# Projections of attention blocks as four products of 32 columns each, on a Trainium2 core

## Chip, cores and metric

The kernel runs on one NeuronCore of a Trainium2 chip, in one launch. The metric is the device time in microseconds (us) from start to end of one execution; several runs of the same kernel are shown with their median. The engines are named as in the profile: PE is TensorE (matrix products; PEld is its loading of weights), DVE is VectorE, ACT is ScalarE, POOL is GpSimd and SP is SyncE, which issues the transfers.

## What is computed

The reference applies four transformer blocks, one after the other, to `x` of 16 batches by 256 tokens by 256 channels, in float32, with 16 heads of 16 channels. A context of 77 tokens a batch serves the cross attentions. The third of the four blocks shows the pattern; the others leave out parts of it or differ in norms, gates, masks and rotary embeddings.

```python
def _L2_xcond_ref(x, c, context, ...):
    shift_a, scale_a, gate_a, shift_m, scale_m, gate_m = split(silu(c) @ W_mod + b_mod, 6)
    qkv = modulate(_ln(x), shift_a, scale_a) @ W_qkv + b_qkv
    ...
    attn_out = softmax(q @ k.T * scale) @ v                 # per batch and head
    x = x + gate_a[:, None] * (attn_out @ W_proj + b_proj)
    q_c = _ln(x) @ W_qc + b_qc                              # cross attention
    k_c, v_c = split(_ln(context) @ W_kvc + b_kvc, 2)
    ...
    x = x + (c_attn_out @ W_cproj + b_cproj)
    h = gelu(modulate(_ln(x), shift_m, scale_m) @ W_mlp1 + b_mlp1)
    return x + gate_m[:, None] * (h @ W_mlp2 + b_mlp2)

x = _L0(x); x = _L1(x); x = _L2(x); x = _L3(x)
```

Block L0 has self attention with rotary embedding and a mask over the 256 by 256 scores, a cross attention and an MLP. L1 is one cross attention. L2 is shown. L3 has rotary embedding in both of its attentions. That makes seven attentions a batch, three self (256 keys) and four cross (77 keys), and three MLPs.

## The kernel before

All of `x` stays in SBUF. The work runs in six stages: attention of L0 (weights "a"), its MLP ("b"), attention of L1 and L2 ("c"), the MLP of L2 ("d"), attention of L3 ("e"), its MLP ("f"). An MLP waits for all exponentials of the attention stage ahead of it.

An attention of one batch goes like this. The norm's result is turned into `xT` (channels on partitions, two chunks of 128 by 256 tokens). Projections follow:

- without rotary embedding, `project_T` (L615) makes queries and keys transposed: for each group `g` of 128 output channels and each chunk `k` of input channels one product of a weight block (128 by 128) with `xT` (128 by 256);
- with rotary embedding, `rotate_tasks` (L652) makes them with tokens on partitions (L671); DVE and POOL rotate them, and `turn_back` (L711) transposes them on PE;
- `mmv` (L782) makes the values, tokens on partitions;
- `residual` (L983) is the product after attention and also the MLP's second product; `nk` is 2 for the first and 8 for the second. It adds to `x` on DVE or POOL.

In cross attentions, keys and values come from the 77 context tokens, so their products are 77 wide or 77 high.

Scores are made twice: rows (L828, L840) for a maximum on DVE, and transposed (L922), from which ACT makes the exponentials `ec` (L936). Both use row tiling: four head pairs lie in the four 32-partition strips, and each strip's product takes 32 rows of the array and 128 columns. The masked ones of L0 also add the mask with 64 by 64 products (L915). The sum of values over keys, `values` (L945), uses the other tiling: the exponentials are the moving operand with 128 (or 77) rows, and the values of a head pair are 32 columns, so four head pairs lie in the four column strips of the array and write the four 32-partition strips of one PSUM bank. Projections, transposes and MLP use the whole array.

Every float32 product shows in the trace as two records (two passes) on PE, each with its weight load.

The order on all engines is written out by a planner before the program is built. `Order.add` takes a task with its engine, an estimated duration, the tasks it depends on, and the buffers (`Hold`s) that it takes and uses; `Order.solve` plays the tasks through in time and starts on each engine what is ready, has room for its buffers and has the best priority. On PE it adds a cost when the kind of task differs from that of the one before:

```python
TURN = {"row": 0.2, "col": 0.13}
...
kind = "row" if ts[0].rp is not None else ts[0].kind
dur += self.TURN.get(kind, 0.2) if kind != mode else 0.0
```

Score tasks count as "row", `values` tasks as "col"; projections have no kind. The product of 128 by 128 by 256 has an estimated duration `MM` of 0.432 us.

Buffers matter for one part of the change. There are eight PSUM banks ("b"), two sets of exponentials ("ec") and two of attention results ("oT"). In `attention`, `open_e` (L895) opens the exponentials of head group `g` and key chunk `kc`; the one with `g` and `kc` both 0 also takes the block's oT, which the later `back` fills and `residual` reads.

Of the kernel before, what the change touches and what calls it, by code (L numbers as in the profile page):

```python
# [17 lines left out]
P = 128  # L18
NT = N // P
NC = D // P  # L20
# [53 lines left out]
class Order:  # L74
# [10 lines left out]
    def add(self, eng, dur, run, deps=(), take=(), use=(), prio=0, rp=None, kind=None, more=0.0,  # L85
            lat=0.0, first=False, mb=0.0):

        t = Task()
        t.more, t.lat, t.first, t.mb = more, lat, first, mb
        t.eng, t.dur, t.run, t.prio, t.rp, t.kind = eng, dur, run, prio, rp, kind  # L90
        t.deps = [d for d in deps if d is not None]
        t.take, t.held = list(take), list(take) + list(use)
        for h in t.held:
            h.users += 1
        t.outs, t.left, t.ready, t.no, t.since = [], len(t.deps), 0.0, len(self.tasks), None
        for d in t.deps:
            d.outs.append(t)
        self.tasks.append(t)
        return t
# [95 lines left out]
def pixart_kernel(ctx: ExitStack, tc: tile.TileContext, x, cond_t, ctx_in, mask_c, mask_s, tables, vecs, rows,  # L195
                  mod0, mod1, mod2, mod3, wa, wb, wc, wd, we, wf, out):
    nc = tc.nc
# [26 lines left out]
    def buf(h, tag=None):  # L224

        return pools[tag or h.tag][h.no]

    def psum(h, *dims):

        t = banks[h.no]  # L230
        return t.rearrange("p (a b) -> p a b", a=dims[0]) if dims else t
# [380 lines left out]
        return s, last, hc  # L612


    def project_T(dst, w, xT):  # L615

        for g in range(NC):
            for k in range(NC):
                nc.tensor.matmul(dst[:, g, :], lhsT=w[:, k, g * P:(g + 1) * P], rhs=xT[:, k, :],
                                 start=(k == 0), stop=(k == NC - 1))  # L620
# [31 lines left out]
    def rotate_tasks(s, key, ws, xT, src_t, n, half, uses, name, prio):  # L652


        nt = (n + P - 1) // P
        r = min(n, P)
        width = len(ws) * D
        out_t, hold = [], []
        for group in ([list(range(nt))] if len(ws) == 1 else [[t] for t in range(nt)]):
            hm, hr, hq, u = Hold("b"), Hold("rope"), Hold("qk"), {}  # L660
            nm = f"{key}_{name}_{group[0]}"
            w_all = len(group) * width

            def mm(group=group, u=u, hm=hm, hq=hq):
                u["p"] = psum(hm)
                u["r1"] = s[key, group[0]] = buf(hq)
                for i, t in enumerate(group):
                    for j, w in enumerate(ws):
                        at = (i * len(ws) + j) * D
                        for k in range(NC):  # L670
                            nc.tensor.matmul(u["p"][0:r, at:at + D], lhsT=xT()[:, k, t * P:t * P + r],  # L671
                                             rhs=w()[:, k, :], start=(k == 0), stop=(k == NC - 1))

            def turns(group=group, u=u, hr=hr):
                r1 = u["r1"]
                r2 = u["r2"] = buf(hr)
                hn = width // HD
                for i, t in enumerate(group):
                    tt = (t * P % half) // P
                    pv, v1, v2 = (a[0:r, i * width:(i + 1) * width].rearrange("q (h w) -> q h w", w=HD)  # L680
                                  for a in (u["p"], r1, r2))
                    cs = tabT[0:r, tt, 0, :].unsqueeze(1).to_broadcast([r, hn, HD])
                    nc.vector.tensor_tensor(v1, pv, cs, ALU.mult)
                    for z in range(2):
                        sn = tabT[0:r, tt, 1, 8 * z:8 * z + 8].unsqueeze(1).to_broadcast([r, hn, 8])
                        nc.vector.tensor_tensor(v2[:, :, 8 * z:8 * z + 8], pv[:, :, 8 - 8 * z:16 - 8 * z], sn,  # L686
                                                ALU.mult)

            def plus(u=u, w_all=w_all):
                r1 = u["r1"][0:r, 0:w_all]  # L690
                nc.gpsimd.tensor_tensor(r1, r1, u["r2"][0:r, 0:w_all], ALU.add)  # L691
            size = len(group) * len(ws)
            a = add("PE", size * NC * MM, mm, deps=[src_t], take=[hm, hq], use=uses, prio=prio)
            d = add("DVE", 0.75 * size, turns, deps=[a, tab_t], take=[hr], use=[hm, hq], prio=prio)
            out_t.append(add("POOL", 0.65 * size, plus, deps=[d], use=[hr, hq], prio=prio))
            hold.append(hq)
        return out_t, hold, nt, r
# [18 lines left out]
    def attention(b, name, n, wv, wkeys, h_w, w_t, eps, mod, half, biases, masked, pre_add, gate, prio, ctxs=None,  # L716
# [31 lines left out]
        if half is None:  # L748
            hm1, hm2, u = Hold("b"), Hold("b"), {}

            def mmq():
                u["q"] = psum(hm1, NC)
                project_T(u["q"], wv[kq], s["xT"])

            def mmk():
                p = psum(hm2)
                u["k"] = p[:, 0:NC * n].rearrange("p (c n) -> p c n", n=n)
                project_T(u["k"], wv[kk], src())
            a = add("PE", (4 * MM) if self_ else 1.0, mmk, deps=[*src_t, w_t[kk], late_t], take=[hm2], use=[h_kq, *h_src, *h_w],
                    prio=prio)  # L760
            k_t = take_k(s, bk, n, lambda: u["k"], a, [hm2, h_kq], prio)
            a = add("PE", 4 * MM, mmq, deps=[xT_t, w_t[kq], late_t], take=[hm1], use=[h_kq, hx, *h_w], prio=prio)
            q_t = take_q(s, bq, lambda: u["q"], a, [hm1, h_kq], prio)
        elif self_:
            info = rotate_tasks(s, "qk", [lambda: wv[kq], lambda: wv[kk]], lambda: s["xT"],
                                add("NO", 0.0, lambda: None, deps=[xT_t, w_t[kq], w_t[kk]], prio=prio), N, half,
                                [hx, *h_w], nm, prio)
            q_t = turn_back(s, "qk", 0, info, lambda *z: take_q(s, None, *z), h_kq, f"q{nm}", prio)
            k_t = turn_back(s, "qk", D, info, lambda *z: take_k(s, None, n, *z), h_kq, f"k{nm}", prio)
        else:  # L770
            info = rotate_tasks(s, "kr", [lambda: wv[kk]], src, add("NO", 0.0, lambda: None, deps=[*src_t, w_t[kk]],
                                                                   prio=prio), n, N, [*h_src, *h_w], nm, prio)
            k_t = turn_back(s, "kr", 0, info, lambda *z: take_k(s, None, n, *z), h_kq, f"k{nm}", prio)
            info = rotate_tasks(s, "qr", [lambda: wv[kq]], lambda: s["xT"],
                                add("NO", 0.0, lambda: None, deps=[xT_t, w_t[kq]], prio=prio), N, half, [hx, *h_w],
                                nm, prio)
            q_t = turn_back(s, "qr", 0, info, lambda *z: take_q(s, None, *z), h_kq, f"q{nm}", prio)
# [4 lines left out]
        def mmv():  # L782
            ps = uv["p"] = psum(hm3)
            xT = src()
            for t in range(nk):
                for k in range(NC):
                    nc.tensor.matmul(ps[0:rows_n, t * D:(t + 1) * D], lhsT=xT[:, k, t * P:t * P + rows_n],  # L787
                                     rhs=wv[kv][:, k, :], start=(k == 0), stop=(k == NC - 1))

        def take_v():  # L790
# [2 lines left out]
            pairs = pairs.rearrange("p t h (a w) -> p t h a w", w=HD)  # L793
            for t in range(nk):
                nc.scalar.copy(pairs[:, t, :, 0:4:3, :], pv[:, t].rearrange("p (h i) w -> p h i w", i=2))
        a = add("PE", nk * NC * MM, mmv, deps=[*src_t, w_t[kv]], take=[hm3], use=[h_v, *h_src, *h_w], prio=prio)
        v_t = add("ACT", 0.37 * nk, take_v, deps=[a, ones_t], use=[hm3, h_v], prio=prio)


# [90 lines left out]
        for g in range(NC):  # L890
            u5, avs, h_av, h_so = {}, [], Hold("b"), Hold("ts")
            for kc in range(nk):
                h_e, ex = Hold("ec"), []

                def open_e(g=g, kc=kc, h_e=h_e):  # L895
                    if g == 0 and kc == 0:
                        s["oT"] = buf(h_ot)
                    for r in range(4):
                        s["e", g, kc, r] = buf(h_e)[:, r]
                t_e = add("NO", 0.0, open_e, deps=[qx_t, v_t, barrier], take=[h_e] if g or kc else [h_e, h_ot],  # L900
                          prio=prio)
                for rp in (1, 0):
                    hs = [Hold("b"), Hold("b")]
# [79 lines left out]
    def residual(s, b, deps, lhsT, w, nk, holds, gate, name, prio, after=None):  # L983
# [3 lines left out]
        for t in range(NT):  # L987
            def mm(t=t):
                if t == 0:
                    u["p"] = psum(hm, NT)  # L990
                for k in range(nk):
                    nc.tensor.matmul(u["p"][:, t, :], lhsT=lhsT(k, t), rhs=w()[:, k, :], start=(k == 0),  # L992
                                     stop=(k == nk - 1))
            ts.append(add("PE", nk * MM, mm, deps=[*deps, *ts], take=[hm] if t == 0 else [],
                          use=holds if t == 0 else [hm, *holds], prio=prio))
        if gate is None:
            def plus():
# [359 lines left out]
```

## Time and profile before

| | |
|---|---|
| time, median of three runs | 2632.84 us (2628.79 to 2638.83) |
| profiled execution: its time, its span | 2631.43 us, 2629.7 us |
| instructions in the span | 56144 |
| granted TensorE clock, mean | 0.995 |
| PE records of scores: L828, L840, L922 | 1536, 2048, 5120 |
| PE records of values: L945 | 5120 |
| PE records of projections with a 128 by 128 weight: L619, L671, L787, L992 | 640, 640, 384, 896 |
| PE records of the MLPs: L1035, L992 | 1536, 1536 |
| ACT exponentials, L936: count, mean of one | 1152, 596 ns |

A line in a list of the trace names the line of the kernel, engine and operation, what is written and read, the size and the count. In the timeline, lines begin with the start and the length of a merged piece; the ends of PE's products are modelled and reach into the next product, so the spacing of starts tells more of PE than its busy time. A line of waits has the total, the number and the longest.

### The profile page before, as it was taken

Reading aid. Unit: us, or ns where it says so; the run is one execution under the profiler, and the core shown is the slowest. Engines: PE = TensorE matmul, PEld = TensorE weight load, DVE = VectorE, ACT = ScalarE, POOL = GpSimd, SP = SyncE. Lnnn points to the kernel's source line nnn. Section 1 sums busy time; section 2 is a strip of 40 time slices with the busy share of each in tenths; the row PEclk is TensorE's granted clock in tenths of the full one; section 3 lists DMA queues with packets and bytes.
Section 4 is the critical chain, followed back from the end, with each engine's and each line's share of the span. In section 5 each row is a group of like instructions: output and inputs, shape, how many; then the busy total and the mean of one; then the engine's idle time right before and its main releaser. Section 6 shows DMA issues by size and latency. Waiting matters only on the chain. (4 is left out here: it accounts for less than half of the span.)

```text
span 2629.7 us, 56144 instructions
## 1 busy us (share of the span) xinstructions
PE 2575.5 (98%) x21512; PEld 1813.2 (69%) x21512; DVE 1627.7 (62%) x4537; ACT 1255.4 (48%) x2511; POOL 1113.5 (42%) x1413
## 2 busy tenths in 40 slices
PE   8999999999999899999999999999999999999999
PEld 5555565666888666666666667888666666666888
DVE  7888886676131577777777775111888887885100
ACT  2444455664333456555556654322455555554322
POOL 5233333558452355233334656442333324657310
PEclk9999999999999899999999999999999999999999
DMA  5000101223321121111111113111100001122110
GB/s 171 30 27 29 34 25 39 73 80 101 100 78 54 40 70 54 48 55 40 39 40 38 61 62 114 64 54 45 35 28 30 28 24 37 50 66 71 56 57 29
DMA packets 159749, 143.10 MB, mean 54 GB/s; under 512 B 24648, under 2 KB 124216, under 8 KB 158712
## 3 DMA queue, kind: packets, MB, share of 16 engines
q1 hardware_dynamic: 159480, 139.51, 16.9%
q8 instruction: 169, 2.77, 0.4%
q14 instruction: 100, 0.82, 0.1%
HBM read 91.86 MB, written 47.61 MB: 53 GB/s over the span
## 5 line engine op out<-in xcount | busy, mean ns | idle before, releaser
L936 ACT ACTIVATE ec<-bank 128x512 f32<-128x512 f32 (+1 forms) x1152 | 608.5, 596 | 514.0 <-PE bank L828 260.7
L922 PE MATMUL bank<-kq 32*128 32x256 f32 (+1 forms) x5120 | 627.9, 395 | 4.8 <-DMA kq<-mrow 4.4
L491 POOL TENSOR_SCALAR xn<-x_sb,mv,rstd 128x256 f32<-128x256 f32 x320 | 451.1, 1464 | 108.4 <-DVE y L519 97.8
L922 PEld LDWEIGHTS bank<-kq 32*128 32x128 f32 (+1 forms) x5120 | 357.2, 167 | 172.8 <-issue 105.1
L828 PE MATMUL bank<-kq 32*128 32x512 f32 x1536 | 432.5, 633 | 2.4 <-ACT ec L936 2.4
L858 DVE TENSOR_REDUCE mx<-bank 128x2 f32<-128x512 f32 x544 | 341.6, 681 | 46.0 <-PE bank L828 43.7
L945 PE MATMUL bank<-ec,v 128*32 128x256 f32 (+1 forms) x5120 | 347.9, 385 | 5.8 <-ACT ec L936 3.6
L1040 ACT ACTIVATE ec<-bank,vec 128x256 f32<-128x256 f32 x384 | 159.7, 467 | 401.3 <-PE bank L1035 373.2
L1035 PE MATMUL bank<-xT,kq 128*128 128x256 f32 x1536 | 341.4, 379 | 0.0
L992 PE MATMUL bank<-kq,ec 128*128 128x256 f32 x1536 | 339.7, 379 | 0.0
L992 PEld LDWEIGHTS bank<-kq,ec 128*128 128x128 f32 x1536 | 291.5, 190 | 39.5
L1035 PEld LDWEIGHTS bank<-xT,kq 128*128 128x128 f32 x1536 | 290.5, 190 | 40.4 <-issue 1.6
L967 POOL TENSOR_TENSOR od<-ts,rec 128x128 f32<-128x128 f32 x448 | 170.1, 402 | 318.7 <-DVE rec L961 318.1
L519 DVE STREAM_TRANSPOSE y<-xn 128x512 f32<-128x512 f32 x158 | 110.9, 702 | 298.9 <-DMA yd<-y 257.6
L945 PEld LDWEIGHTS bank<-ec,v 128*32 128x32 f32 (+1 forms) x5120 | 137.2, 109 | 183.0 <-issue 75.5
L862 DVE TENSOR_REDUCE mx<-bank 128x4 f32<-128x308 f32 x512 | 211.9, 468 | 55.4 <-PE bank L922 25.3
L466 POOL TENSOR_SCALAR rstd<-mv 128x2 f32<-128x2 f32 x160 | 37.5, 235 | 423.8 <-DVE mv L461 347.7
L854 DVE CUSTOM_DVE_ANT_0 junk<-bank,ctx 128x256 f32<-128x256 f32 x448 | 188.8, 421 | 45.2 <-PE bank L828 12.2
L954 DVE STREAM_TRANSPOSE ts<-bank 128x512 f32<-128x512 f32 x224 | 158.3, 707 | 76.6 <-PE bank L945 69.1
L691 POOL TENSOR_TENSOR qk<-qk,rope 128x512 f32<-128x512 f32 (+1 forms) x96 | 112.9, 1178 | 194.4 <-DVE rope L686 151.3
L1008 POOL TENSOR_TENSOR x_sb<-x_sb,tmp 128x512 f32<-128x512 f32 x80 | 101.6, 1270 | 179.4 <-DVE tmp L1005 179.2
L840 PE MATMUL bank<-kq 32*128 32x154 f32 x2048 | 167.1, 308 | 1.5 <-DVE ts L954 0.5
(164 smaller groups left out, 3437.8 us busy)
## 6 DMA issues: line engine op xcount, KB each, us to landing
yd<-y SPq DMA_DIRECT2D x158, 256.0 KB
xr<-yd SPq DMA_DIRECT2D x158, 256.0 KB
kq<-in_mod_dram SPq DMA_DIRECT2D x10, 512.0 KB
cin<-in_ctx_in_dram SPq DMA_DIRECT2D x36, 128.0 KB
x_sb<-in_x_dram SPq DMA_DIRECT2D x16, 256.0 KB
gb<-gate_g0m SPq DMA_DIRECT2D x16, 256.0 KB
gb<-gate_g2a SPq DMA_DIRECT2D x16, 256.0 KB
gb<-gate_g2m SPq DMA_DIRECT2D x16, 256.0 KB
```

Source lines behind the costliest of these rows:

```text
L491: nc.gpsimd.tensor_scalar(to, of, s["mv"][:, t, 0:1], s["rstd"][:, t:t + 1], ALU.subtract, ALU.mult)
L828: ls.append(lambda ps=ps, R=R, keys=keys: nc.tensor.matmul(ps.rearrange("p (s k) -> p s k", k=N), lhsT=s["qx"][R, 0, g, t * P:(t + 1) * P] ...
L840: ls.append(lambda ps=ps, R=R, keys=keys, tt=tt: nc.tensor.matmul(ps[:, 2 * tt * n:2 * (tt + 1) * n].rearrange("p (s k) -> p s k", k=n), l ...
L854: nc.vector.tensor_tensor_reduce(junk, u[i][:, i2 * N:(i2 + 1) * N], mb[:, t, :], -1.0, 3.0e38, ALU.add, ALU.min, m[:, i2, g, t:t + 1])
L858: nc.vector.tensor_reduce(m[:, :, g, t], u[i].rearrange("p (s k) -> p s k", k=N), AX.X, ALU.max, negate=True)
L862: nc.vector.tensor_reduce(m[:, :, g].rearrange("p s t -> p t s"), u[i][:, 0:4 * n].rearrange("p (t s k) -> p t s k", s=2, k=n), AX.X, ALU. ...
L922: (lambda ps=u[i], R=R, q=q: nc.tensor.matmul(ps[0:rows_n, q * N:(q + 1) * N], lhsT=s["kz"][R, q, g, kc * P:kc * P + rows_n], rhs=s["qx"][ ...
L936: nc.scalar.activation(e, u[i][0:rows_n], AF.Exp)
L945: nc.tensor.matmul(u5["p"][32 * r:32 * r + 32, 1 - q, :], lhsT=s["v"][0:rows_n, kc, 8 * g + 2 * r + 1 - q, :], rhs=s["e", g, kc, r][0:rows ...
L967: nc.gpsimd.tensor_tensor(ov[:, :, HD * i:HD * i + HD], ts[:, i, :, HD * i:HD * i + HD], rec[:, i, :].unsqueeze(2).to_broadcast([P, N // 3 ...
L992: nc.tensor.matmul(u["p"][:, t, :], lhsT=lhsT(k, t), rhs=w()[:, k, :], start=(k == 0), stop=(k == nk - 1))
L1035: nc.tensor.matmul(u["p"][:, j, :], lhsT=wv["w1"][:, k, f * P:(f + 1) * P], rhs=s["xT"][:, k, :], start=(k == 0), stop=(k == NC - 1))
```

## The change

Projections with a full set of 128 columns in the attention blocks are made as four products of 32 columns each, in the four column strips that `values` uses. The new helper `strips` runs over the chunks of input channels (`pairs`), and within each over the four slices `J` of 32 columns of the stationary operand; each writes its 32 partitions of the same destination. It is called in `project_T` (except for keys of the 77 context tokens), in `rotate_tasks` (except for these), in `mmv` for self attention, and in `residual` for attention (`nk == NC`). The products with 77 tokens, the transposes and the MLPs stay as they are.

The tasks concerned get `kind="col"`, so the planner counts 0.13 us for them instead of 0.2 after a task of another kind and nothing after one of values.

Last, every `open_e` now takes the block's oT with its exponentials, and sets it, whichever comes first.

```diff
+    def strips(dst, pairs):
+
+        for k, (l, r) in enumerate(pairs):
+            for J in (slice(32 * j, 32 * j + 32) for j in range(4)):
+                nc.tensor.matmul(dst[J], lhsT=l[:, J], rhs=r, start=(k == 0), stop=(k == len(pairs) - 1))
+
-    def project_T(dst, w, xT):
+    def project_T(dst, w, xT, small=False):
 
         for g in range(NC):
+            if not small:
+                strips(dst[:, g, :], [(w[:, k, g * P:(g + 1) * P], xT[:, k, :]) for k in range(NC)])
+                continue
             for k in range(NC):
                 nc.tensor.matmul(dst[:, g, :], lhsT=w[:, k, g * P:(g + 1) * P], rhs=xT[:, k, :],
                                  start=(k == 0), stop=(k == NC - 1))
...
+                        if r == P:
+                            strips(u["p"][:, at:at + D], [(xT()[:, k, t * P:(t + 1) * P], w()[:, k, :]) for k in range(NC)])
+                            continue
...
-            a = add("PE", size * NC * MM, mm, deps=[src_t], take=[hm, hq], use=uses, prio=prio)
+            a = add("PE", size * NC * MM, mm, kind="col" if r == P else None, deps=[src_t], take=[hm, hq], use=uses, prio=prio)
...
-            a = add("PE", 4 * MM, mmq, deps=[xT_t, w_t[kq], late_t], take=[hm1], use=[h_kq, hx, *h_w], prio=prio)
+            a = add("PE", 4 * MM, mmq, kind="col", deps=[xT_t, w_t[kq], late_t], take=[hm1], use=[h_kq, hx, *h_w], prio=prio)
...
+                if self_:
+                    strips(ps[:, t * D:(t + 1) * D], [(xT[:, k, t * P:(t + 1) * P], wv[kv][:, k, :]) for k in range(NC)])
+                    continue
...
-                    if g == 0 and kc == 0:
-                        s["oT"] = buf(h_ot)
+                    s["oT"] = buf(h_ot)
...
-                t_e = add("NO", 0.0, open_e, deps=[qx_t, v_t, barrier], take=[h_e] if g or kc else [h_e, h_ot],
+                t_e = add("NO", 0.0, open_e, deps=[qx_t, v_t, barrier], take=[h_e, h_ot],
...
+                if nk == NC:
+                    strips(u["p"][:, t, :], [(lhsT(k, t), w()[:, k, :]) for k in range(nk)])
+                    return
```

The tasks of `mmk`, `mmv` and `residual` get their kind in the same way.

More of the change, by code (lines that the diff above doesn't have):

```diff
@@ L757, in mmk @@
                 u["k"] = p[:, 0:NC * n].rearrange("p (c n) -> p c n", n=n)
-                project_T(u["k"], wv[kk], src())
-            a = add("PE", (4 * MM) if self_ else 1.0, mmk, deps=[*src_t, w_t[kk], late_t], take=[hm2], use=[h_kq, *h_src, *h_w],
+                project_T(u["k"], wv[kk], src(), not self_)
+            a = add("PE", (4 * MM) if self_ else 1.0, mmk, kind="col" if self_ else None, deps=[*src_t, w_t[kk], late_t], take=[hm2], use=[h_kq, *h_src, *h_w],
                     prio=prio)
             k_t = take_k(s, bk, n, lambda: u["k"], a, [hm2, h_kq], prio)
-            a = add("PE", 4 * MM, mmq, deps=[xT_t, w_t[kq], late_t], take=[hm1], use=[h_kq, hx, *h_w], prio=prio)
+            a = add("PE", 4 * MM, mmq, kind="col", deps=[xT_t, w_t[kq], late_t], take=[hm1], use=[h_kq, hx, *h_w], prio=prio)
             q_t = take_q(s, bq, lambda: u["q"], a, [hm1, h_kq], prio)
@@ L795, in take_v @@
                 nc.scalar.copy(pairs[:, t, :, 0:4:3, :], pv[:, t].rearrange("p (h i) w -> p h i w", i=2))
-        a = add("PE", nk * NC * MM, mmv, deps=[*src_t, w_t[kv]], take=[hm3], use=[h_v, *h_src, *h_w], prio=prio)
+        a = add("PE", nk * NC * MM, mmv, deps=[*src_t, w_t[kv]], take=[hm3], kind="col" if self_ else None, use=[h_v, *h_src, *h_w], prio=prio)
         v_t = add("ACT", 0.37 * nk, take_v, deps=[a, ones_t], use=[hm3, h_v], prio=prio)
@@ L993, in mm @@
                                      stop=(k == nk - 1))
-            ts.append(add("PE", nk * MM, mm, deps=[*deps, *ts], take=[hm] if t == 0 else [],
+            ts.append(add("PE", nk * MM, mm, deps=[*deps, *ts], take=[hm] if t == 0 else [], kind="col" if nk == NC else None,
                           use=holds if t == 0 else [hm, *holds], prio=prio))
```

## The prediction

> **What bounds the kernel now.** I read the page's busy times first, then the busy times by stage, then who PE waits for, and last the timeline of PE alone.
>
> ```profile
> PE 2575.5 (98%) x21512; PEld 1813.2 (69%) x21512; DVE 1627.7 (62%) x4537; ACT 1255.4 (48%) x2511; POOL 1113.5 (42%) x1413
> ```
>
> PE is busy for 98% of the span; nothing else passes 69%. The three attention stages (about 30 to 650, 870 to 1640 and 1850 to 2420 us) are where the change acts, and there the next engine has room:
>
> ```profile
> 40.00:640.00 600.00, 591.33 (x5845) 359.31 (x5844) 471.09 (x1682) 310.49 (x570) 249.17 (x330) 1.00 0.16 48
> 880.00:1630.00 750.00, 736.87 (x7165) 490.42 (x7166) 551.78 (x1371) 432.12 (x882) 347.74 (x471) 0.99 0.18 55
> 1860.00:2410.00 550.00, 537.65 (x5149) 347.08 (x5148) 450.11 (x1131) 295.56 (x562) 244.62 (x331) 1.00 0.13 39
> ```
>
> Columns after the window's length: PE, PEld, DVE, ACT, POOL. PE is at 98 to 99%, DVE at 79, 74 and 82%, ACT near 55%. PE's listed waits are small; the longest in total are
>
> ```profile
> PE bank L619 <- ACT xT L539: 8.0, 1, 8.0
> PE bank L382 <- DMA kq<-in_mod_dram: 4.8, 2, 4.2
> PE bank L922 <- DMA kq<-mrow: 4.4, 3, 2.5
> ```
>
> and all of PE's idle time is 2629.7 - 2575.5 = 54 us. So what PE does, and how it goes from one thing to the next, sets the end. Busy time hides that second part, since ends are modelled and overlap the next start. Start times (first column of the timeline) show it:
>
> ```profile
> 1044.06 1.99 PE L619 MATMUL bank<-xT,w_c 128*128 128x256 f32 x8
> 1045.98 1.07 PE L945 MATMUL bank<-ec,v 77*32 77x256 f32 x16
> 1046.98 1.99 PE L992 MATMUL bank<-w_c,oT 128*128 128x256 f32 x8
> 1048.82 1.03 PE L787 MATMUL bank<-w_c,ctx 128*77 128x256 f32 x4
> ...
> 1055.05 1.09 PE L787 MATMUL bank<-w_c,ctx 128*77 128x256 f32 x4
> 1056.07 0.44 PE L922 MATMUL bank<-kq 32*77 32x256 f32 x2
> ...
> 1084.66 1.93 PE L945 MATMUL bank<-ec,v 77*32 77x256 f32 x32
> 1086.52 1.99 PE L828 MATMUL bank<-kq 32*128 32x512 f32 x15
> ...
> 1756.92 7.07 PE L1035 MATMUL bank<-xT,kq 128*128 128x256 f32 x32
> 1763.82 6.42 PE L992 MATMUL bank<-kq,ec 128*128 128x256 f32 x29
> ...
> 2384.16 1.10 PE L922 MATMUL bank<-kq 32*77 32x256 f32 x16 [2.46 <-DMA kq<-mrow]
> ```
>
> Each float32 product stands as two records (passes). Three readings:
> - In the MLP, where nothing changes shape, 32 passes of 128x128 by 256 take 1763.82 - 1756.92 = 6.90 us: 0.216 us a pass.
> - A projection (L619: four products, 8 passes) between other shapes takes 1045.98 - 1044.06 = 1.92 us, where 8 x 0.216 is 1.73. A run of the full array costs 0.19 to 0.20 us beyond its passes. The trace's start times split that: 0.320 instead of 0.216 to the second pass, and 0.309 instead of 0.216 from the last pass to the first of another shape. I use 0.197.
> - The values (L945: 32 columns, four strips side by side) take 1.00 us for 16 records and 1.86 us for 32. The difference, 0.86 us for 16 records, is 0.216 for four strips: **four products of 32 columns cost exactly what one of 128 columns costs.** Beyond its passes a run of strips costs 1.00 - 0.863 = 0.137 us.
>
> **What the Trainium skill says.** "TensorEngine Tiling (Array Packing)", section Key Properties, says that changing the tiling mode drains TensorE and that tiles load weights and multiply in parallel. The trace agrees with both: the 0.309 for 0.216 at each change, and the four strips of a pass beginning some 7 ns apart. "TensorE: Matmul & The Clock Gate", section Part 2, says that the sequencer may spend about 62 ns on each MATMUL. The trace of before speaks against that as a bound (below, under the slower rival), but no run here keeps up strips for more than 32 records.
>
> **The change part by part.**
>
> *Projections as strips.* Those concerned are L619, L671, L787 and L992 with operands 128*128 by 256, except where the MLP calls L992 with eight k-steps: 640 + 640 + 384 + 896 = 2560 passes. Each becomes four records, so PE gets 7680 more matmuls and as many weight loads. At 0.216 us a pass either way the steady cost is nil. For this I have the values as the nearest row: same columns, same 256 elements, same rows (128 for self attention). What differs is that the four strips read one and the same moving operand; the values' four read four tensors.
>
> *Runs.* The two built programs differ in how often the shape changes, which I counted from the order of PE's instructions. Runs of the full array: 422 before, 204 after. Runs of strips: 312 and 413. Row-tiled runs (scores): 494 and 500; runs on 64x64: 127 and 128. Of the full runs 254 begin with a 128-column pass before, 20 after (nearly all MLP and its surroundings); the other 168, and 184 after, begin with transposes or the 77-wide context products, which stay on the full array. Such a short run costs about 0.15 beyond its passes (L787 x4: 1056.07 - 1055.05 = 1.02, less 4 x 0.216 = 0.864).
> - Before: 254 x 0.197 + 168 x 0.15 + 312 x 0.137 = 50.0 + 25.2 + 42.7 = 117.9 us.
> - After: 20 x 0.197 + 184 x 0.15 + 413 x 0.137 = 3.9 + 27.6 + 56.6 = 88.1 us.
> - Seven more row and 64x64 runs at about 0.18: +1.3 us.
>
> Sum: 29.8 - 1.3 = **28.5 us less PE time.** Its pieces: a projection that stands alone goes from 1.92 to 1.86 us; one that meets the values saves a whole change (1.92 + 1.00 = 2.92 becomes 12 x 0.216 + 0.137 = 2.73), and some 190 of the new strip runs hold both. Against it, a projection that used to join a transpose or a 77-wide product in one run of the full array now stands apart and costs about 0.1 more; the run counts contain that.
>
> *The planner's new costs* (`kind="col"`) move instructions on all engines: the order differs on PE from the first rows on, and on SP, ACT, POOL and DVE too. No instruction is added there (DVE 4146 rows in both, SP 719, POOL 1034). Such a reshuffle changes PE's waits: the 54 us listed, and short waits for banks inside row runs, which the modelled ends hide. I can bound it only by size: 12 us either way, a fifth of the listed idle time. I take 0.
>
> *The oT edit.* Each opening of an exponential buffer now also needs the block's oT (two exist). This waits on no engine by itself; behind it stand that block's transposed scores on PE, the exponentials on ACT, and then its values. Before, the third block could start a later chunk while both oT were held; now it can't. Put into the kernel before alone, the edit shifts PE's order from row 1233 of 7103 on and leaves its changes of shape nearly equal (1354 and 1361). Between -3 and +8 us; I take +1.
>
> *What is late next.* With 28 us less PE work in about 1940 us of attention, DVE's share in the third stage rises from 82 to 83%. Where PE already waits for a bank, the saving turns into a longer wait. By the start times, runs last some 5% longer in all, over the attention stages, than the shortest run of the same content; allowing for bursts of DVE I let 15 to 20% of the saving be lost: +5 us.
>
> Sum on the profiled execution (span 2629.7, time 2631.43): 2631.4 - 28.5 + 1 + 5 = 2608.9. The median of the runs shown is 1.4 us above it (2632.84), so 2610.
>
> **Rivals.** About 0.5% (13 us) is what a measurement here can tell from no change.
> - *A, forecast:* fewer runs, most of it kept: 2610, own range 2598 to 2619. Chance 0.68.
> - *B, the waits shrink too.* A planner with strip runs at 0.13 and nothing at a join plans with what the hardware does; if the reshuffle also takes a dozen us of waits: 2610 - 5 - 12 = 2593. Nothing in the profile favours it, hence 0.10.
> - *C, taken back.* DVE at 82% is an average; in dense stretches PE waits for banks that DVE or ACT empties, and there projections were cover. If two thirds of the saving returns as waits: 2632.8 - 9.5 = 2623. For it: the many short row waits. Against it: DVE's own longest idle times end with PE's scores, so PE feeds DVE, not the reverse. 0.13.
> - *D, slower: strips as projections run slower than 0.216 us a pass,* because PE isn't fed eight instructions in that time (27 ns each) or because one moving operand is read four times at once. Price: 2560 passes times the excess; 11 ns cancels the gain, 16 ns makes the kernel slower by 0.5%, and 62 ns a MATMUL (0.248 a pass) would give 2632.8 - 28.5 + 82 = 2686. For it: merged runs reach 80 records, more than any now. Against it: the last line of the timeline, 16 row-tiled records after a wait of 2.46 us, runs at full pace from its first record, and 32 strips in a row show no gap. 0.09.
>
> That the change doesn't do what it says is excluded by the order: every such projection stands as 32x256 x16.
>
> **How the numbers follow.** The time is A's, 2610. Faster by over 0.5% (under 2619.7): A, B and a little of C, 0.80. Within: most of C and edges of A and D, 0.12. Slower: D, 0.08. The range 2592 to 2630 takes in A, C and half of B and leaves out D.
>
> **What would show it.** PE matmul records rise from 21512 by 7680 to about 29192; a lone projection takes 1.86 us from start to next start, and one with values 2.73; MLP stretches stay at 6.90 us for 32. The attention stages together shrink by 20 to 28 us, MLP by none. It is wrong if strip groups of projections start over 0.22 us apart (D), or if they keep the pace while PE's idle time grows by over 10 us (C).

## The result and the profile after

| | before | changed |
|---|---|---|
| median | 2632.84 us | 2623.18 us (7 runs, 2616.51 to 2629.7) |
| ratio to before, 95% interval | | 0.9959 [0.9943, 0.9976] |
| span of the profiled execution | 2629.7 us | 2618.4 us |

The change makes the kernel 0.41% faster, by 10.8 us. Forecast were 23 us (2610). The time lies within the wide range of the prediction, but the gain is less than half of the forecast, and under the 0.5% from which the prediction calls a kernel faster; it had given 0.12 to a change that small.

From the page of the changed kernel, the busy times and the transfers of instructions:

```profile
PE 2562.5 (98%) x29192; PEld 1673.9 (64%) x29192; DVE 1623.3 (62%) x4537; ACT 1259.0 (48%) x2511; POOL 1117.5 (43%) x1413
...
q8 instruction: 229, 3.75, 0.6%
```

The records are the 21512 + 7680 foreseen. From its timeline of PE (start, length, line, tiles, count):

```profile
1040.70 1.93 PE L619 MATMUL bank<-xT,w_c 128*32 128x256 f32 x32
1042.45 1.05 PE L959 MATMUL bank<-ec,v 77*32 77x256 f32 x16
1043.43 0.44 PE L936 MATMUL bank<-kq 32*77 32x256 f32 x2
...
1049.81 1.93 PE L619 MATMUL bank<-xT,w_c 128*32 128x256 f32 x32
1051.56 1.05 PE L959 MATMUL bank<-ec,v 77*32 77x256 f32 x16
1052.43 1.91 PE L619 MATMUL bank<-xT,w_c 128*32 128x256 f32 x32
1054.16 1.91 PE L619 MATMUL bank<-w_c,xT 128*32 128x256 f32 x32
1055.88 1.91 PE L619 MATMUL bank<-w_c,oT 128*32 128x256 f32 x32
...
1077.73 1.94 PE L619 MATMUL bank<-xT,w_c 128*32 128x256 f32 x32
1079.59 0.44 PE L936 MATMUL bank<-kq 32*77 32x256 f32 x2
```

A projection alone takes 1079.59 - 1077.73 = 1.86 us; one with values 1043.43 - 1040.70 = 2.73; inside a run the next projection starts after 1.73 = 8 x 0.216. All three are the forecast's numbers to the last digit, so the strips keep their pace and PE's runs got as short as they should. The lost time is elsewhere. PE's listed waits (total, number, longest) do not name it either; the largest of the changed kernel are

```profile
PE bank L619 <- ACT xT L539: 13.1, 4, 8.1
PE bank L959 <- ACT ec L950: 5.5, 8, 1.9
PE bank L382 <- DMA kq<-in_mod_dram: 4.6, 2, 4.1
PE bank L619 <- DVE oT L985: 4.0, 5, 2.5
```

and its whole idle time is 2618.4 - 2562.5 = 56 us, against 54. So neither sign that the prediction named for C and D is there. Start times place the loss: from the first to the last score the three attention stages take 590.2, 697.6 and 559.0 us, against 596.0, 715.4 and 550.7. The first two are 24 us shorter, the third is 8 us longer; together they shrink by 15 us, where 20 to 28 were forecast.

Most of the 8 us of the third stage is the clock. In three stretches of it the trace of the changed kernel has PE at half its clock (the window, its length, PE's busy time and records, the granted clock, then DMA):

```profile
1880.20:1886.90 6.70, 6.70 (x51) 0.50 0.12 42
2347.80:2354.60 6.80, 4.96 (x48) 0.50 0.06 18
2378.60:2381.90 3.30, 3.30 (x33) 0.50 0.24 84
```

and a projection in the first of them takes 1886.23 - 1882.81 = 3.42 us instead of 1.73:

```profile
1882.81 3.64 PE L619 MATMUL bank<-w_e,oT 128*32 128x256 f32 x32
1886.23 1.42 PE L959 MATMUL bank<-ec,v 128*32 128x256 f32 x16
```

Half of these 17 us is lost, 8.5 us; the third stage of the kernel before has one such stretch, of 3.4 us, and loses 1.7:

```profile
2385.40:2388.70 3.30, 3.04 (x7) 0.50 0.27 91
```

Without the lost halves the third stage takes 550.5 us against 549.0. It did not get longer, but it saved nothing. The prediction took the clock of before, 0.995, for given; how much the clock costs in the median is worked out after the experiments.

### The profile page after: what moved, and what is told of

Its sections match the earlier page's. It is cut to its first block, busy times and chain, and to the rows that moved or that the text cites. A ratio compares the mean times of both kernels' runs of the same rounds, so it can differ in the third digit from the quotient of the medians.

```text
span 2618.4 us, 71534 instructions
## 1 busy us (share of the span) xinstructions
PE 2562.5 (98%) x29192; PEld 1673.9 (64%) x29192; DVE 1623.3 (62%) x4537; ACT 1259.0 (48%) x2511; POOL 1117.5 (43%) x1413
## 3 DMA queue, kind: packets, MB, share of 16 engines
q8 instruction: 229, 3.75, 0.6%
## 4 chain that ended last, share of the span: by engine, by line
PE 91%; DVE 3%; DMA 2%; POOL 2%; ACT 2%; issue 1%; SPq 0%; DVEq 0%; ACTq 0%; POOLq 0%
PE bank L619 21%; PE bank L936 14%; PE bank L1052 13%; PE bank L1009 13%; PE bank L959 11%; PE bank L843 8%; PE bank L855 2%; PE bank L802 2%; PE bank L723 2%; PE bank L628 2%; PE bank L929 2%; POOL xn L491 1%; DMA xr<-yd 1%; ACT ec L950 1%; DVE mx L877 1%
## 5 line engine op out<-in xcount | busy, mean ns | idle before, releaser
L936 PE MATMUL bank<-kq 32*128 32x256 f32 (+1 forms) x5120 | 643.0, 397 | 4.4 <-ACT ec L948 2.0
L843 PE MATMUL bank<-kq 32*128 32x512 f32 x1536 | 448.0, 636 | 1.2 <-ACT ec L950 0.9
L959 PEld LDWEIGHTS bank<-ec,v 128*32 128x32 f32 (+1 forms) x5120 | 155.1, 110 | 159.2 <-issue 37.5
```

The costliest lines, as they stand in the source:

```text
L843: ls.append(lambda ps=ps, R=R, keys=keys: nc.tensor.matmul(ps.rearrange("p (s k) -> p s k", k=N), lhsT=s["qx"][R, 0, g, t * P:(t + 1) * P] ...
L936: (lambda ps=u[i], R=R, q=q: nc.tensor.matmul(ps[0:rows_n, q * N:(q + 1) * N], lhsT=s["kz"][R, q, g, kc * P:kc * P + rows_n], rhs=s["qx"][ ...
L959: nc.tensor.matmul(u5["p"][32 * r:32 * r + 32, 1 - q, :], lhsT=s["v"][0:rows_n, kc, 8 * g + 2 * r + 1 - q, :], rhs=s["e", g, kc, r][0:rows ...
```

## The experiments

Each time is the median of several runs; ratios are to the kernel before, timed on the same chip, with 95% intervals. "By the arithmetic" is the prediction's: runs of one shape, counted in the order of PE's instructions, times their cost beyond the passes. The letters R, C, O, L, P and W stand for the theories that the expectations name.

**Products and order apart.** Two runs cross the two halves of the change. The first (e1) keeps the order of before and makes strips; the kinds and the oT edit are left out (against the changed kernel, in part):

```diff
-            a = add("PE", 4 * MM, mmq, kind="col", deps=[xT_t, w_t[kq], late_t], ...)
+            a = add("PE", 4 * MM, mmq, deps=[xT_t, w_t[kq], late_t], ...)
...
-                    s["oT"] = buf(h_ot)
+                    if g == 0 and kc == 0:
+                        s["oT"] = buf(h_ot)
```

> Strips for all projections concerned, but without the kinds and without the oT edit: every engine's order is that of the kernel before. Runs of one shape on PE: full array 207, strips 406, rows 494, 64x64 127, so by the arithmetic of the prediction 30 us less PE time than before. Theory R (the new order, not the strips, brought the added waits): nearly all of it shows, 2600 to 2608. Theory C (a faster PE turns its saving into waits for banks that DVE and ACT empty, in whatever order): about the changed kernel's time, 2618 to 2626. Theory O (the oT edit makes the waits): as R.

2609.64 us, 0.9914 [0.9899, 0.9929]: just above the range of R and O, and far from C.

The second (e2) keeps the new order and makes whole products:

```diff
         for k, (l, r) in enumerate(pairs):
-            for J in (slice(32 * j, 32 * j + 32) for j in range(4)):
-                nc.tensor.matmul(dst[J], lhsT=l[:, J], rhs=r, start=(k == 0), stop=(k == len(pairs) - 1))
+            nc.tensor.matmul(dst, lhsT=l, rhs=r, start=(k == 0), stop=(k == len(pairs) - 1))
```

> The changed kernel's order (kinds and oT edit) with the projections as whole products of 128 columns, as before. Runs on PE: full array 426, strips 311, rows 500, so the arithmetic gives 2 us more than before. R: the order's waits come on top, 2643 to 2655. C: PE is as slow as before, so no new waits: 2632 to 2638. O: as R.

2657.82 us, 1.0096 [1.0075, 1.0117]: above even the upper end of R and O, and not C. With the same products the new order costs 25 us, of which the arithmetic explains 2; some 10 us go with a lower clock (below).

The busy times on the pages of the strips in the old order, and then of the new order with whole products:

```profile
PE 2554.6 (98%) x29192; PEld 1678.4 (64%) x29192; DVE 1623.5 (62%) x4537; ACT 1253.9 (48%) x2511; POOL 1115.4 (43%) x1413
```

```profile
PE 2603.5 (98%) x21512; PEld 1826.0 (69%) x21512; DVE 1625.3 (61%) x4537; ACT 1257.8 (47%) x2511; POOL 1114.1 (42%) x1413
```

The first issues the same products as the changed kernel, yet there PE is "busy" 8 us longer (2562.5), although its profiled execution had the higher clock (0.993 against 0.991). Busy time hides short waits: a wait shorter than the modelled tail of a product counts as busy (the MLP stretch of before stands as 7.07 us long, and the next starts after 6.90). The second does the work of before and is busy 28 us longer than it (2575.5); more than half of this goes with the clock, 0.988 against 0.995.

**The oT edit.** Alone in the kernel before (e3):

> The kernel before with the oT edit alone (full array 415, strips 314, rows 506 runs: 1 us more by the arithmetic). O: 2643 to 2652. R, with the kinds as the cause: 2631 to 2637. C: 2633.

2647.24 us, 1.0052 [1.0037, 1.0068]: 14 us slower, as O says. With strips and without kinds (e11):

> The changed kernel without the kinds: strips and the oT edit, the planner still counting 0.2 us before a projection. Runs: full 207, strips 407, rows 506, 64x64 127: 28 us less than before by the arithmetic. If the oT edit costs with strips what it costs without (14 us) and the kinds nothing, 2617 to 2625, as the changed kernel. If costs that fit the strips help the plan, the time is longer than the changed kernel's: 2626 to 2636.

2627.88 us, 0.9984 [0.9975, 0.9992]. Against the strips in the old order (0.9914) the edit costs 0.7%, 18 us, 2 of them by the arithmetic. The second expectation holds: without the kinds the time is longer than the changed kernel's. By start times the third attention stage is 15 us longer (557.7 against 543.1 us), of which lost halves of the clock make 3.

Is it the wait for one of two oTs? Two runs on the changed kernel take that away, one with the oT taken later (e4),

```diff
-                t_e = add("NO", 0.0, open_e, deps=[qx_t, v_t, barrier], take=[h_e, h_ot],
+                t_e = add("NO", 0.0, open_e, deps=[qx_t, v_t, barrier], take=[h_e],
...
-            done.append(add("DVE", 0.45, back, deps=[a], use=[h_so, h_ot], prio=prio))
+            done.append(add("DVE", 0.45, back, deps=[a], take=[h_ot], use=[h_so], prio=prio))
```

> The changed kernel, but a block takes its oT where it is first written (at the turn back of its first head group) instead of with its exponentials. Runs on PE: full array 203, strips 414, rows 501. O: the lost time comes back, 2603 to 2612. R with the kinds as the cause, and C: 2618 to 2628, as the changed kernel.

and one with `"oT": 3` in `CAPS` (e5):

> The changed kernel with its oT edit as it is, but three oT buffers instead of two. PE's instructions then stand in the order of the run with the late oT. If what the edit costs is the wait of a block's opening for one of two oTs, the third takes it away: 2605 to 2614. If the edit costs something else (its place in the plan, the buffer's address), it stays at 2618 to 2628.

2609.38 us, 0.9918 [0.9898, 0.9938], and 2611.67 us, 0.9909 [0.9892, 0.9925]: in both the lost time comes back, 11 and 13 us of the changed kernel's. The order on PE is the same in the two, so they test one order and not two. Loads of PE's weights that waited, in the third stage of the changed kernel and of the one with three oTs:

```profile
PEld bank L959 <- ACT ec L950: 9.6, 15, 2.4
```

```profile
PEld bank L959 <- ACT ec L950: 6.4, 15, 0.7
```

The same number of waits of the values for exponentials, but a longest of 2.4 us against 0.7 and 3 us less in all: this is a part of the 9 us by which the third stage is shorter (549.7 against 559.0; 2 of them are the clock).

The same late oT in the kernel before (e6), and with strips but no kinds (e12):

> The kernel before, with the late oT and nothing else (no strips, no kinds). In the kernel before, 41 of 112 blocks open a later chunk first while both oTs are held, so it mostly escapes the wait already. If so, the late oT brings it little: 2624 to 2634. If the hold of oT still costs it as much as the edit does (14 us), 2615 to 2620.

> Strips and the late oT, no kinds. Runs: full 194, strips 402, rows 497, 64x64 127: 32 us less than before by the arithmetic. If the late oT costs here what it cost in the kernel before (18 us), 2614 to 2622; if the late oT is free with strips, as it seemed with the kinds, 2602 to 2610.

2651.11 us, 1.0064 [1.0048, 1.0080], above every expectation, and 2617.92 us, 0.9950 [0.9931, 0.9968], in the first range of its expectation. So without the kinds the late oT costs as much as the edit in the kernel before (17 us against 14), and about half of it with strips (9 against 18, each against e1). That the wait for oT is the whole cause falls.

**Is any new order bad?** Two nudges to the planner of before, `MM = 0.436` (e9) and `LAG = 0.14` (e10):

> The kernel before with the planner's estimate for a product at 0.436 us instead of 0.432; nothing else. The order changes from early on, the runs on PE hardly (full 422, strips 312, rows 503, 64x64 126: 1 us more by the arithmetic). Theory L (the order of before is an unusually good one among the orders that the planner makes, and any reshuffle costs): 2640 to 2655. Theory O (it is the oT edit): 2630 to 2638.

> The kernel before with the planner's lag between engines at 0.14 us instead of 0.13; nothing else. Runs: full 427, strips 311, rows 506, 64x64 127: 2 to 3 us more by the arithmetic. L: 2642 to 2655. O: 2632 to 2639.

2631.14 us, 1.0002 [0.9988, 1.0015], and 2637.67 us, 1.0021 [1.0012, 1.0031]. L does not hold for these two: the orders differ from early on and cost 0 and 6 us, of which the arithmetic gives 1 and 3. Two nudges are few, so they do not show how wide orders of this planner scatter.

**Opening out of order.** One thing that e3, e6 and the changed kernel share against before is that no block opens a later chunk first, where 41 did. With that rule given back (e13), and in longer runs besides (e14):

> Strips and kinds with the rule of before for oT: only a block's first opening takes it, later chunks may open ahead of it; where a head group is turned back first, that takes it. 45 of 112 blocks then open a later chunk first. Runs: full 211, strips 414, rows 513, 64x64 127: 25 us less than before by the arithmetic. If opening out of order is what the edit took away (theory P), 2598 to 2609. If only a third oT or a late one helps (theory W, the wait for one of two oTs), the first chunk still waits: 2612 to 2622.

> As the former, and the planner's choice on PE prefers the kind it is at by 20 points. Runs: full 186, strips 409, rows 493, 64x64 128: 33 us less than before by the arithmetic. P: 2592 to 2604. W: 2606 to 2616.

2635.68 us, 1.0007 [0.9993, 1.0021], and 2631.65 us, 0.9993 [0.9983, 1.0003]. P falls; W expected less than was measured too. With kinds, the rule of before is the worst of the three (this, the edit, the late oT), also after allowing for its low clock.

**Longer runs.** On the late-oT kernel, the planner's choice for PE prefers the kind it is at, by 20 points (e7) and by 40 (e8):

```diff
-cand.sort(key=lambda t: (t.prio, t.no) if eng == "PE" else ...
+cand.sort(key=lambda t: (t.prio - 20 * (("row" if t.rp is not None else t.kind) == mode), t.no) if eng == "PE" else ...
```

> The late-oT kernel, and the planner's choice on PE prefers a task of the kind it is at by 20 points of priority (two blocks). Runs: full 186, strips 392, rows 488, 64x64 128; the arithmetic gives 8 us less than with the late oT: 2601 if the waits stay, 2605 to 2620 if a block's delay costs as much as the runs saved.

> As the former with 40 points (four blocks). Runs: full 166, strips 348, rows 457, 64x64 126; the arithmetic gives 23 us less than with the late oT: 2586 if the waits stay. If theory C is right for a denser PE, half or more of it returns as waits for banks that DVE and ACT empty: 2597 to 2615.

2606.74 us, 0.9901 [0.9883, 0.9920], and 2614.31 us, 0.9931 [0.9916, 0.9946]. With 20 points the time falls by some 4 us of the 8, which the intervals don't tell from none; with 40 all of the 23 us are given back, at the upper end of C's numbers. That does not single out C, since the 40 points also rewrite the order. The first is the fastest version seen, not told apart from the late oT or the third one.

**The granted clock, and the planner's own time.** The executions of one kernel differ in their mean granted clock, and their time follows it: over the 261 executions of all kernels on record it is 2.2 us longer for each 0.001 less, and scatters by only 1.6 us around that line. The mean clock also differs from kernel to kernel. The table gives it, and the time against before as measured and as the line puts it at equal clock (to 1 or 2 us). The last column is the end time that the planner computes for its own order, against that of before; it stands only where the planner counts with costs that fit the products of that kernel, and with the `MM` and `LAG` of before.

| kernel | mean clock | measured, us | at equal clock, us | planner's end, us |
|---|---|---|---|---|
| before (108 executions) | 0.9944 | 0 | 0 | 0 |
| e1, strips in the order of before | 0.9925 | -23 | -27 | |
| e2, whole products in the new order | 0.9900 | +25 | +15 | |
| e3, oT edit alone | 0.9938 | +14 | +12 | +19 |
| e6, late oT alone | 0.9925 | +17 | +13 | +13 |
| e9, `MM = 0.436` | 0.9933 | +1 | -2 | |
| e10, `LAG = 0.14` | 0.9935 | +6 | +4 | |
| e11, strips and oT edit | 0.9924 | -4 | -9 | |
| e12, strips and late oT | 0.9933 | -13 | -16 | |
| changed | 0.9913 | -11 | -17 | -10 |
| e4, changed with late oT | 0.9917 | -22 | -29 | -31 |
| e5, changed with three oTs | 0.9914 | -24 | -30 | -31 |
| e7, e4 with 20 points | 0.9930 | -26 | -29 | -25 |
| e8, e4 with 40 points | 0.9897 | -18 | -28 | -12 |
| e13, changed with the rule of before | 0.9897 | +2 | -9 | -8 |
| e14, e13 with 20 points | 0.9900 | -2 | -11 | -22 |

Two things follow. At equal clock the oT edit still costs 12 us alone, 18 with strips (e11 against e1) and 11 to 13 with strips and kinds (changed against e4 and e5), and the 40 points neither cost nor bring anything (e8 against e4). And the planner, before anything was run, put 19 us on the oT edit and 13 on the late oT. Beside e1 the same two cost 18 and 11 us at equal clock. In its plan PE is idle for 119 us in the order of before, for 133 with the edit and 131 with the late oT, and in the third stage for 38, 46 and 45. So the waits lie in the planned order itself. It is no sure guide: for the longer runs (e8, e14) it is off by 16 and 11 us.

## Why the prediction came out as it did

| same order, strips against whole products | arithmetic | measured ratio | at equal clock |
|---|---|---|---|
| order of before (e1 / before) | -30.5 us | 0.9914 [0.990, 0.993] | -27 us |
| changed order (changed / e2) | -30.5 us | 0.9864 [0.984, 0.989] | -33 us |
| oT edit, no kinds (e11 / e3) | -29.2 us | 0.9932 [0.991, 0.995] | -22 us |
| late oT, no kinds (e12 / e6) | -32.2 us | 0.9887 [0.986, 0.991] | -30 us |

(The last three ratios are quotients of those above, their intervals combined in quadrature.)

- *The bound and the price of a run:* right. At a fixed order strips bring 0.7 to 1.4%, 27 us on average of 30.6 by the arithmetic.
- *Strips at 0.216 us a pass:* right. D is out (see the last section).
- *What is late next,* 5 us of 28.5 lost: near in size on average (4 of 30.6), but single orders bring from 18 to 36 us, and no run traces the loss to DVE.
- *The oT edit, +1 within -3 to +8, and the planner's new costs, 0 within 12:* **this step failed.** In the order of before the strips bring 27 us at equal clock; the changed kernel brings 17. The new order takes 10 us, of which the few more runs explain 2. The oT edit is what costs: 12 us alone and 18 with strips. The kinds earn some of it back (changed against e11: 8 us at equal clock).
- *The granted clock* **has no term in the sum,** and the prediction gives no reason for leaving it out. It fell from 0.9944 to 0.9913 in the mean, which at 2.2 us for 0.001 is some 7 us (from 7 executions of the changed kernel, so give or take 2).
- *The sum with what was measured:* -27 for strips instead of -28.5 + 5, +10 for the order instead of +1, +7 for the clock instead of nothing: 10 us less than before, 2623. The strips brought a little more than forecast, and that hid a part of the two misses.
- *Why the edit was mis-sized:* I judged it by the number of shape changes, which it hardly moves (1354 to 1361), and by the absence of a new instruction. It decides when a block's exponentials may start, and behind them stand PE's second scores, ACT and the values, as I wrote; I gave that chain no price. The planner plays this chain through, and its end time, which the prediction does not use, has 19 us for the edit and -10 for the whole change.
- *Rival C* has the measured 2623 as its number, by luck. Its mechanism had the place wrong: e1, with the faster PE in the old order, keeps its saving. What came back did so through the new order and the clock.

What stays open: which dependence in the planned order makes the added waits. The wait for one of two oTs explains 11 to 13 us with strips and kinds, and nothing in the kernel before, where taking oT late costs 17; opening out of order does not explain it. Open too is why the clock fell. The seven kernels with a mean clock under 0.992 all have the kinds, e2 with its whole products among them, so it is not the strips alone. Whether the waits of the new order bring the stretches of low clock was not tested; if they do, the order's part is larger than 10 us.

## What to carry to other kernels

Price a change of array shape by start times, not by busy times: here it cost 0.197 us for a run of the full array and 0.137 for one of strips, and counting such runs in the built order gave the gain at a fixed order to some 15% on average, though a single order could be off by 40%. Where a planner writes the order, an edit to what a task must hold is a change of its own: build the order with and without it, read the planner's own end time for both, and run the two halves apart before adding them up. A small correction beside the main change can cost more than half of what the change earns, and one more buffer may buy it back. And before explaining a difference of 0.5%, look at the granted clock of both kernels: here it was worth two thirds of the gain that was measured.

## What the hardware showed beyond expectation

PE took four weight loads and four products every 0.216 us, 27 ns an instruction on average, over 144 records in a row: the four projections and one sum of values that begin at 1049.81 us in the timeline shown, 112 of them in 1055.88 - 1049.81 = 6.07 us, although before no strips had run for more than 32 records, and the prediction looked for at most 80. That is 54 ns for a load and its product, below the 62 ns a product of rival D. The instructions' own transfers rose from 2.77 to 3.75 MB without a trace in PE's pace. The four strips reading one moving operand cost the same, 0.216 us a pass, as four reading different ones.
